# The second feed-forward product as two 64-row halves, between five groups of scores

## The chip, the cores and the metric

One core of a Trainium2 chip runs the whole kernel. The metric is the device time of one execution in microseconds (us), as the median of several runs; lower is better.

## The reference, cut to what matters

The input x is 16 batches of 512 rows of 256 numbers. Each row is normalised (xn). One branch is an attention layer with 16 heads whose scores are a position table, two per-row terms and a small content product; it is followed by a layer norm, a feed-forward network and a second layer norm. The other branch is a gated network whose inputs and weights are rounded to a 4-bit grid. The output is x plus the product of the two branches.

```python
attn = softmax(where(causal, table + qm + km + MIX * qc @ kc.T / sqrt(8), -1e9))
h    = _ln(xn + (attn @ v) @ out_w + out_b, ln1_g, ln1_b)
ffn  = gelu(h @ ffn_w1 + ffn_b1) @ ffn_w2 + ffn_b2     # 256 -> 1024 -> 256
s    = _ln(h + ffn, ln2_g, ln2_b)
g    = silu(fp4_linear(silu(fp4_linear(xn, w_gate)) * fp4_linear(xn, w_up), w_down))
out  = x + s * g
```

The change concerns `gelu(...) @ ffn_w2 + ffn_b2`: a product over 1024 contraction rows.

## The kernel before, in words

After a preamble the work is a loop over 64 steps: 16 batches `b` times four groups `g` of four heads. Line numbers are those of the profile; nearly every instruction carries L72, the line of the helper that records it, so groups are told apart by the names of their tiles.

**What a step does.** Step (b, g) multiplies the weights of the previous step's heads with v (`context`, tile `cp`, L502), then computes, in five bursts, the scores that become the weights of its own four heads (`weights`, tiles `ws`, L466) and the scores whose row maxima the following step needs (`maxima`, tiles `ms`, L427). After the bursts come the gate and up products of one tile of 128 rows of the gated branch (`hidden`, tiles `gp`, `up`, `gu`, L655), the turning of the maxima (`subtracted`, tile `mp`, L442) and the down product of the tile before (`gate`, tile `dp`, L693).

**The batch before rides along.** In steps g = 0 and 1 the previous batch's attention output is projected (`output`, L530). In g = 1 and 2 the first feed-forward product of one half of its rows (two tiles of 128) follows the down product: `expand` (L592) writes eight tiles `act` of 128 hidden units. In g = 2 and 3 `contract` (L603) multiplies them with `w2`: for each of two row tiles, eight products over 128 contraction rows each, all into one PSUM bank `f2` that `biased` (L285) has filled with the bias by a product of ones. `added` (L522) then adds the bank to h on the vector engine and takes the row statistics; `finish` (L621) normalises and writes the output.

**The two sorts of scores.** A score product contracts 36 or 38 rows, so two heads sit in the tensor engine at once, one in rows 0 to 63 and one in rows 64 to 127 (`scores`, L413), each into its own bank. All other products named here use all 128 rows.

**PSUM.** Of the eight banks two belong to a pool `ps_s` with one buffer (the pair `ws`, and later `gu`), one to `cp`, and five to a pool that everything else takes from, in program order and oldest release first. A bank comes free when its reader has run: the vector engine for `ms` (a masked maximum, tile `junk`), `f2` and `up`; the scalar engine for the transposed tiles `xqtp`, `hqtp`, `htp`, which it copies out, and for `gp`, `f1` and `dp`.

**The order.** The order on the tensor, vector and scalar engines is the program's, held by dependencies; only DMA issues and GpSimd are ordered by the scheduler. The program's order within a step is written out in `PLAN` (L711), one string for each g. `W` is a burst of `ws` scores with its exponential on the scalar engine (and a multiplication by the table on GpSimd); `V` is the same with its own two banks of the common pool, one for each head; `M` issues a burst of `ms` scores; `!` puts the maxima of all open `M` and all postponed additions on the vector engine; `f` is two of the sixteen 128-row products of `contract`; `x`, `y` and `h` are transposes of the gated branch's input, its hidden tile (in two parts) and h. The two strings that matter:

```python
"WVM!ffWMM!ffxWM!ffWM!ffyyh", "WMV!ffWMM!ffxWM!fffWM!yfy"   # g = 2 and g = 3
```

Of the kernel before, what the change touches and what calls it, by code (L numbers as in the profile page):

```python
# [17 lines left out]
ALU = mybir.AluOpType  # L18
# [4 lines left out]
B, S, D = 16, 512, 256  # L23
H, M, W, R = 16, 16, 8, 8
# [4 lines left out]
P = 128  # L29
# [21 lines left out]
def tile_block(ctx: ExitStack, tc: tile.TileContext, a: dict, pos: bass.AP, win: bass.AP, out: bass.AP):  # L51
# [22 lines left out]
    pe, dve, act = InOrder(nc.tensor, True), InOrder(nc.vector, False), InOrder(nc.scalar, False)  # L74
# [31 lines left out]
    def statistics(mv, src):  # L106

        st = sb.tile([P, nc.vector.BN_STATS_DIM], F32, name="st", tag="st", bufs=2)
        dve.bn_stats(st, src)
        dve.bn_aggr(mv, st)  # L110

    def inverse_deviation(rs, var):
        nc.gpsimd.tensor_scalar(rs, var, LN_EPS, None, ALU.add)
        nc.gpsimd.tensor_tensor(rs, rs, mhalf[:, : rs.shape[1]], ALU.pow)
# [30 lines left out]
    def layernorm(src, mean, rs, gain, bias):  # L145

        dve.scalar_tensor_tensor(src, src, mean, gain, ALU.subtract, ALU.mult)
        dve.scalar_tensor_tensor(src, src, rs, bias, ALU.mult, ALU.add)
# [29 lines left out]
    NF = D_FF // P  # L178
    w1 = keep.tile([P, NC, D_FF], F32, name="w1", tag="w1")
    w2 = keep.tile([P, NF, D], F32, name="w2", tag="w2")  # L180
    fb1 = keep.tile([P, NF], F32, name="fb1", tag="fb1")

    sums = keep.tile([P, P], F32R, name="sums", tag="sums")
    rows = keep.tile([P, 2, D], F32R, name="rows", tag="rows")
# [61 lines left out]
    def bank(name):  # L246
        return ps.tile([P, 512], F32, name=name, tag="mm")

    mm = pe.matmul

    def turn(dst, src, one=ident):
        pe.transpose(dst, src, one)
# [20 lines left out]
    later = []  # L273

    def caught_up():
        while later:
            later.pop(0)()
# [4 lines left out]
        ((0, 0, 0),), ((1, 0, 0),), ((0, 1, 0), (0, 3, 384)), ((1, 1, 0), (1, 3, 384)), ((0, 2, 0), (1, 2, 256))  # L282
    )

    def biased(acc, i, tiles=2):  # L285

        mm(
            acc[:, : tiles * D].rearrange("p (t d) -> p t d", t=tiles), sums,
            rows[:, i, :].unsqueeze(1).to_broadcast([P, tiles, D]),
            start=True, stop=False, skip_group_check=True,  # L290
        )

    def rows_of(tiles, t):

        return tiles[t // 2][:, t % 2, :]
# [226 lines left out]
    def added(h, tiles, acc, mv):  # L522

        half, at = tiles[0] // 2, tiles[0] % 2
        flat = h[half][:, at : at + len(tiles), :].rearrange("p t d -> p (t d)")
        dve.tensor_tensor(flat, acc[:, : len(tiles) * D], flat, ALU.add)
        for t in tiles:
            statistics(mv[:, t, :], rows_of(h, t))

    def output(b, h, cts, half, mv):  # L530

        cTs, ops = {}, []

        def normal(t):
            tp = bank(f"ctp_{b}_{t}").rearrange("p (h s) -> p h s", s=SLOT)
            for g in range(H // 4):
                turn(tp[:, 4 * g : 4 * g + 4, :].rearrange("p h s -> p (h s)"), cts[g][:, t * P : (t + 1) * P])
            rinv = sb.tile([P, H], F32, name=f"rinv_{b}_{t}", tag="rinv", bufs=2)
            dve.reciprocal(rinv, tp[:, :, HD])
            cx = sb.tile([P, H, HD], F32, name=f"cx_{b}_{t}", tag="cx", bufs=3)  # L540
            dve.tensor_tensor(cx, tp[:, :, 0:HD], rinv.unsqueeze(2).to_broadcast([P, H, HD]), ALU.mult)
            return cx.rearrange("p h d -> p (h d)")

        def turned(t, cx):
            t2 = bank(f"ct2_{b}_{t}")
            for c in range(NC):
                turn(t2[:, c * P : (c + 1) * P], cx[:, c * P : (c + 1) * P])
            cTs[t] = sb.tile([P, D], F32, name=f"cT_{b}_{t}", tag="cx", bufs=3)
            act.copy(cTs[t], t2[:, :D])

        def product(t):
            acc = bank(f"op_{b}_{t}")
            op = acc[:, :D]
            biased(acc, 0, 1)
            cT = cTs[t]
            for c in range(NC):
                mm(op, cT[:, c * P : (c + 1) * P], wo[:, c, :], start=False, stop=(c == NC - 1), skip_group_check=True)
            later.append(lambda: added(h, (t,), acc, mv))

        first, second = 2 * half, 2 * half + 1  # L560
        cx = normal(first)
        yield 0.43
        cx2 = normal(second)
        yield 0.43
        turned(first, cx)
        yield 0.21
        turned(second, cx2)
        yield 0.21
        product(first)
        yield 0.96  # L570
        product(second)
        yield 0.96
# [10 lines left out]
    def turned_h(b, h, half):  # L583
        hT = sb.tile([P, NC, 2 * P], F32, name=f"hT_{b}_{half}", tag="hT")
        tp = bank(f"htp_{b}_{half}")
        for c in range(NC):
            for t in range(2):
                turn(tp[:, (2 * c + t) * P : (2 * c + t + 1) * P], rows_of(h, 2 * half + t)[:, c * P : (c + 1) * P])
        act.copy(hT.rearrange("p c t -> p (c t)"), tp)
        return hT  # L590

    def expand(b, half, hT):  # L592

        acts = []
        for f in range(NF):
            fp = bank(f"f1_{b}_{half}_{f}")
            for c in range(NC):
                mm(fp[:, : 2 * P], w1[:, c, f * P : (f + 1) * P], hT[:, c, :], start=(c == 0), stop=(c == NC - 1))
            acts.append(sb.tile([P, 2 * P], F32, name=f"act_{b}_{half}_{f}", tag="act", bufs=NF + 2))
            act.activation(acts[f], fp[:, : 2 * P], AF.Gelu, bias=fb1[:, f : f + 1])  # L600
        return acts

    def contract(b, h, half, acts, mv, together=2):  # L603

        for first in range(2 * half, 2 * half + 2, together):
            tiles = tuple(range(first, first + together))
            acc = bank(f"f2_{b}_{first}")
            biased(acc, 1, together)
            for i, t in enumerate(tiles):
                at = (t % 2) * P  # L610
                for f in range(NF):
                    mm(
                        acc[:, i * D : (i + 1) * D], acts[f][:, at : at + P], w2[:, f, :],
                        start=False, stop=(f == NF - 1), skip_group_check=True,
                    )
                    if t == tiles[-1] and f == NF - 1:
                        later.append(lambda tiles=tiles, acc=acc: added(h, tiles, acc, mv))
                    if f % 2:
                        yield 0.88

    def finish(b, h, half, mv, gated):  # L621

# [85 lines left out]
        ("r|px|rpp|p|yyr", "pp"),  # L708
        ("p|x||yytt|tt", ""),
    )  # L710
    PLAN = ("WMc!llWM!xWM!ccllyWMlyW!M!l", "WMll!kWM!lWM!xllyhWMccy!WM!l", "WVM!ffWMM!ffxWM!ffWM!ffyyh", "WMV!ffWMM!ffxWM!fffWM!yfy")  # L711

    def keeping(b, g):
        kept(b, g)
# [129 lines left out]
    for c in range(3):  # L844
        at = slice(32 * c, 32 * c + H)
# [148 lines left out]
    for k in range(H // 2 + 2):  # L994
# [20 lines left out]
        if k > 1:  # L1015
            i = k - 2
            row = 2 * M * (i % 4)
            for e in range(2):
                mm(
                    cp[row : row + 2 * M, :], amp[:, 2 * i + e, :], sines[i][:, e, :],  # L1020
                    start=(e == 0), stop=(e == 1), skip_group_check=True,
# [82 lines left out]
    waiting, hq, cts, turned_hs, acts, coming, mv = None, None, [], {}, {}, None, None  # L1104
# [7 lines left out]
    for s in range(STEPS):  # L1112
        b, g = divmod(s, H // 4)
        old, has_old = b - 1, b > 0
# [9 lines left out]
        if has_old:  # L1124
            if g % 2 == 0:
                mv = sb.tile([P, NT, 2], F32, name=f"mv{1 + g // 2}_{old}", tag=f"mv{1 + g // 2}")
# [8 lines left out]
            }  # L1135
            plan = PLAN[g].split("|")
        else:
# [10 lines left out]
        for letter in "".join(part if set(part) & set("WV") else "WM" + "!" * ("!" not in part) + part for part in plan):  # L1148
            if letter in "WV":
                k = next(weighed)  # L1150
# [70 lines left out]
    old = B - 1  # L1221
    h, gated = xns[old], gates[old]
    x_last = load_x(old)
    context(*waiting)
    kept(*waiting[:2])
    mv = sb.tile([P, NT, 2], F32, name="mv1_last", tag="mv1")
    hand = [output(old, h, cts, half, mv) for half in range(2)] + [turned_hidden(*before, hq)]
    for i in (0, 0, 1, 1, 0, 0, 1, 1, 0, 2, 0, 2):
        next(hand[i])
# [11 lines left out]
    mv = sb.tile([P, NT, 2], F32, name="mv2_last", tag="mv2")  # L1241
    for half in range(2):
        acts[half] = expand(old, half, hT)
        if half == 0:
            hT = turned_h(old, h, 1)
        for i, _ in enumerate(contract(old, h, half, acts[half], mv, 1)):
            if i % 4 < 3:
                continue
            caught_up()
            t = 2 * half + i // 4  # L1250
            rs = sb.tile([P, 2], F32, name=f"rs_last_{t}", tag="rs2")
            inverse_deviation(rs[:, :1], mv[:, t : t + 1, 1])
            layernorm(rows_of(h, t), mv[:, t, 0:1], rs[:, :1], g2, b2)
            gt = gated[:, t, :]
            dve.tensor_tensor(gt, gt, rows_of(h, t), ALU.mult)
            dve.tensor_tensor(gt, gt, x_last[:, t, :], ALU.add)
            nc.sync.dma_start(out=out[old, t * P : (t + 1) * P, :], in_=gt)
# [43 lines left out]
```

## Time and profile before

| | |
|---|---|
| Median of 3 runs | 1875.72 us (1874.68 to 1876.05) |
| Profiled execution: span from the first to the last instruction | 1872.6 us |
| Between span and median | 3.1 us |
| PE (tensor engine) busy | 1774.8 us, 95% |
| DVE (vector engine) busy | 1423.1 us, 76% |
| POOL (GpSimd) busy | 1310.3 us, 70% |
| ACT (scalar engine) busy | 1069.1 us, 57% |
| Mean granted clock of the tensor engine | 0.973 |

The profiled execution is known by its span alone; the 3.1 us are what lies around it if it ran as the median did. A single-precision product is two MATMUL passes in the trace, so 16 products show as x32; the scores' type needs one pass. A pass's listed duration is from its issue to the modelled end of its last result, longer than the step from one pass to the next, so the pace of a stage is read from the starts. PEld are the loads of the stationary operand.

The loop is very regular. The steps g = 2 and g = 3 with a previous batch occur 15 times each, the first from 286.5 us, and one of each, at 712.52 and at 741.70 us, is shown below.

### The profile page before, as it was taken

What the parts mean: (1) busy time and instruction counts of PE and PEld (TensorE: products, weight loads), DVE (VectorE), ACT (ScalarE), POOL (GpSimd) and SP (SyncE); (2) the same over time, 40 slices, a digit from 0 to 9 for tenths busy, and PEclk for the clock granted to TensorE, in tenths of its full rate; (3) what the DMA queues carried; (4) which work ended last, traced back from release to release, by engine and by line L of the source; (5) the groups of instructions that cost most, each with busy time, mean ns of one, the idle gap of its engine ahead of it and who ended that gap; (6) DMA issues with size and microseconds to landing.
All of it is one profiled execution on the core that took longest, in us unless ns stands there. A gap on an engine that the chain in (4) does not pass through costs nothing.

```text
span 1872.6 us, 31762 instructions
## 1 busy us (share of the span) xinstructions
PE 1774.8 (95%) x10411; PEld 1240.5 (66%) x10411; DVE 1423.1 (76%) x3887; ACT 1069.1 (57%) x1853; POOL 1310.3 (70%) x1128
## 2 busy tenths in 40 slices
PE   5679799999999999999999999999999999999998
PEld 2235467676776767676776767677676767677676
DVE  5878587787878777787878777787878778787754
ACT  5654455655665555556565565556555565565553
POOL 5467477767776776777676776777677776777671
PEclk8869799999999999999999999999999999999999
DMA  6344242432323242422334242332333242232200
GB/s 203 95 148 134 81 129 68 138 87 88 109 89 120 68 126 80 137 84 76 112 95 127 60 135 81 117 101 76 112 94 109 73 138 86 77 108 79 72 21 12
DMA packets 127114, 184.68 MB, mean 99 GB/s; under 512 B 15315, under 2 KB 57749, under 8 KB 126949
## 3 DMA queue, kind: packets, MB, share of 16 engines
q1 hardware_dynamic: 122496, 181.25, 32.2%
q8 instruction: 83, 1.36, 0.3%
q10 hardware_dynamic: 4004, 0.98, 0.3%
q14 instruction: 83, 0.67, 0.1%
q0 software_dynamic: 448, 0.42, 0.1%
HBM read 136.45 MB, written 45.09 MB: 97 GB/s over the span
## 4 chain that ended last, share of the span: by engine, by line
PE 81%; DVE 8%; POOL 1%; issue 1%; ACT 1%; DMA 0%; DVEq 0%; POOLq 0%; ACTq 0%
PE f L72 25%; PE dp L72 8%; PE gu L72 8%; PE cp L72 7%; PE ws L72 5%; DVE junk L72 4%; PE op L72 4%; PE gp L72 4%; PE up L72 4%; PE ms L72 4%; PE vp L72 3%; PE hqtp L72 2%; DVE cx L72 1%; PE qk_wk L72 1%; PE qk_wq L72 1%
## 5 line engine op out<-in xcount | busy, mean ns | idle before, releaser
L500 POOL TENSOR_TENSOR pr<-pr,table 128x1024 f32<-128x1024 f32 (+2 forms) x448 | 768.0, 1748 | 75.2 <-ACT pr L72 73.0
L72 DVE CUSTOM_DVE_ANT_0 junk<-ms,mask 128x512 bf16<-128x512 f32 (+3 forms) x1024 | 501.9, 490 | 231.9 <-PE ms L72 155.0
L72 ACT ACTIVATE pr<-ws 128x1024 f32<-128x1024 f32 (+1 forms) x350 | 327.0, 955 | 134.4 <-PE ws L72 129.1
L72 ACT ACT_TABLE_LOAD x168 | 215.5, 1283 | 64.3 <-PE gp L72 48.8
L72 PE MATMUL f<-w,act 128*128 128x256 f32 x1024 | 249.0, 387 | 0.0
L72 PE MATMUL f<-hT,w 128*128 128x256 f32 x1024 | 226.3, 380 | 0.0
L72 PEld LDWEIGHTS f<-hT,w 128*128 128x128 f32 x1024 | 194.8, 190 | 26.3 <-ACT hT L72 0.2
L72 PEld LDWEIGHTS f<-w,act 128*128 128x128 f32 x1024 | 187.0, 190 | 31.3
L232 POOL TENSOR_TENSOR wide<-wide,scale 128x704 f32<-128x704 f32 (+1 forms) x71 | 96.6, 1361 | 136.5 <-DVE wide L72 132.9
L72 PE MATMUL ws<-qT,kT 38*128 38x512 f32 (+3 forms) x1024 | 157.5, 371 | 21.4 <-ACT pr L72 16.5
L72 PE MATMUL dp<-wdT,hqT 128*128 128x256 f32 x768 | 176.2, 379 | 0.0
L72 PEld LDWEIGHTS dp<-wdT,hqT 128*128 128x128 f32 x768 | 146.1, 190 | 31.1 <-issue 6.7
L72 ACT ACTIVATE act<-f,fb 128x256 f32<-128x256 f32 x256 | 118.2, 474 | 75.3 <-PE f L72 72.5
L72 PE MATMUL ms<-kT,qT 36*128 36x512 f32 (+3 forms) x1024 | 145.1, 330 | 9.5 <-DMA kT<-k_d 6.3
L72 PE MATMUL cp<-pr,va 128*17 128x512 f32 (+3 forms) x2048 | 151.5, 434 | 0.0
L72 PEld LDWEIGHTS ws<-qT,kT 38*128 38x128 f32 x1024 | 81.6, 188 | 90.8 <-issue 51.7
L72 PEld LDWEIGHTS cp<-pr,va 128*17 128x17 f32 x2048 | 54.3, 97 | 99.4 <-issue 79.5
L223 POOL TENSOR_SCALAR scale<-amax 128x32 f32<-128x32 f32 (+1 forms) x104 | 37.0, 356 | 116.6 <-DVE amax L72 113.5
L72 DVE TENSOR_TENSOR wide<-wide,m 128x704 f32<-128x704 f32 (+2 forms) x126 | 112.4, 892 | 4.1
L222 POOL TENSOR_TENSOR wide<-wide,inv 128x704 f32<-128x704 f32 (+1 forms) x71 | 99.1, 1396 | 21.5 <-DVE inv L72 21.1
L72 PEld LDWEIGHTS ms<-kT,qT 36*128 36x128 f32 x1024 | 96.2, 189 | 18.4 <-issue 12.8
L72 DVE TENSOR_SCALAR m<-m 128x512 f32<-128x512 f32 (+1 forms) x104 | 102.6, 986 | 3.4
(217 smaller groups left out, 3009.5 us busy)
## 6 DMA issues: line engine op xcount, KB each, us to landing
table<-rv SPq DMA_DIRECT2D x64, 1024.0 KB
kT<-k_d SPq DMA_DIRECT2D x256, 76.0 KB
qT<-q_d SPq DMA_DIRECT2D x256, 72.0 KB
x<-in_L_attn_x_dram SPq DMA_DIRECT2D x21, 512.0 KB
q_d<-q_hi SPq DMA_DIRECT2D x32, 256.0 KB
q_d<-q_lo SPq DMA_DIRECT2D x32, 256.0 KB
k_d<-k_hi SPq DMA_DIRECT2D x32, 256.0 KB
k_d<-k_lo SPq DMA_DIRECT2D x32, 256.0 KB
```

Of the source, the lines that this page charges most:

```text
L72: return lambda *args, **kw: self.follow(op(*args, **kw))
L222: nc.gpsimd.tensor_tensor(blocks(dst), blocks(src), per_block(inv), ALU.mult)
L223: nc.gpsimd.tensor_scalar(scale, amax, 1.0 / 6.0, 1e-12, ALU.mult, ALU.max)
L232: nc.gpsimd.tensor_tensor(blocks(dst), blocks(dst), per_block(scale), ALU.mult)
L500: nc.gpsimd.tensor_tensor(part, part, table[:, mine, j * P :], ALU.mult)
```

## The change

`contract` splits each of its products in two along the contraction: rows 0 to 63 into one bank, rows 64 to 127 into a second, in turn. The bias product contracts 64 rows (the rows that hold the bias are among them) and goes into the first bank; the first upper product starts the second. So a step has 32 products of 64 rows in two banks in place of 16 of 128 in one. `added_halves` adds both banks to h, one vector instruction for each, and then takes the statistics as before. The plans of g = 2 and 3 lose `V`, and have four groups `ff` of eight half products between five groups `WM!`; all transposes stand at the end. The last batch's tail keeps whole products, in a function of its own.

```diff
-    def biased(acc, i, tiles=2):
+    def biased(acc, i, tiles=2, n=P):
         mm(
-            acc[:, : tiles * D].rearrange("p (t d) -> p t d", t=tiles), sums,
-            rows[:, i, :].unsqueeze(1).to_broadcast([P, tiles, D]),
+            acc[:, : tiles * D].rearrange("p (t d) -> p t d", t=tiles), sums[:n],
+            rows[:n, i, :].unsqueeze(1).to_broadcast([n, tiles, D]),
             start=True, stop=False, skip_group_check=True,
         )
...
+    def added_halves(h, half, acc, mv):
+        flat = h[half].rearrange("p t d -> p (t d)")
+        for part in acc:
+            dve.tensor_tensor(flat, part, flat, ALU.add)
+        for t in (2 * half, 2 * half + 1):
+            statistics(mv[:, t, :], rows_of(h, t))
...
-    def contract(b, h, half, acts, mv, together=2):
-        for first in range(2 * half, 2 * half + 2, together):
-            tiles = tuple(range(first, first + together))
-            acc = bank(f"f2_{b}_{first}")
-            biased(acc, 1, together)
-            for i, t in enumerate(tiles):
-                at = (t % 2) * P
-                for f in range(NF):
+    def contract(b, h, half, acts, mv):
+        tiles = (2 * half, 2 * half + 1)
+        acc = [bank(f"f2_{b}_{half}_{upper}") for upper in range(2)]
+        biased(acc[0], 1, 2, 64)
+        for i, t in enumerate(tiles):
+            for f in range(NF):
+                for upper in range(2):
+                    k = slice(64 * upper, 64 * upper + 64)
                     mm(
-                        acc[:, i * D : (i + 1) * D], acts[f][:, at : at + P], w2[:, f, :],
-                        start=False, stop=(f == NF - 1), skip_group_check=True,
+                        acc[upper][:, i * D : (i + 1) * D], acts[f][k, i * P : (i + 1) * P], w2[k, f, :],
+                        start=(upper == 1 and i == 0 and f == 0), stop=(f == NF - 1), skip_group_check=True,
                     )
-                    if t == tiles[-1] and f == NF - 1:
-                        later.append(lambda tiles=tiles, acc=acc: added(h, tiles, acc, mv))
-                    if f % 2:
-                        yield 0.88
+                if t == tiles[-1] and f == NF - 1:
+                    later.append(lambda: added_halves(h, half, acc, mv))
+                if f % 2:
+                    yield 0.88
...
-    PLAN = (..., "WVM!ffWMM!ffxWM!ffWM!ffyyh", "WMV!ffWMM!ffxWM!fffWM!yfy")
+    PLAN = (..., "WM!ffWM!ffWM!ffWM!ffWM!xyyh", "WM!ffWM!ffWM!ffWM!ffWM!xyy")
```

In the built program the changed step has this order on the tensor engine: cp; then ws, ms, bias and eight half products; three times ws, ms and eight half products; ws, ms; then xqtp, hqtp (four transposes and two), in g = 2 htp, and gp. The waits that the build attaches to the transposes behind the last burst are: the first of hqtp for the scalar engine (its bank is the one that xqtp leaves), the fifth of hqtp and the first of htp for the vector engine (the two banks of the last `ms`); gp waits in g = 2 for the scalar engine (the bank of the first hqtp) and in g = 3 for the vector engine (the second bank of the last `ms`). The order of the other engines is the same but for the added addition, the one exponential that replaces the two of `V`, the place of the copy of xqtp, which now follows the last exponential, and, in the DMA queue of SP, one load of `kT` for each batch (the last of the group g = 1), which moves from behind the first output store of step g = 3 to ahead of the four small writes of the maxima (L454).

More of the change, by code (lines that the diff above doesn't have):

```diff
@@ L601, in expand, with contract_tile @@
         return acts
-    def contract(b, h, half, acts, mv, together=2):
-        for first in range(2 * half, 2 * half + 2, together):
-            tiles = tuple(range(first, first + together))
-            acc = bank(f"f2_{b}_{first}")
-            biased(acc, 1, together)
-            for i, t in enumerate(tiles):
-                at = (t % 2) * P
-                for f in range(NF):
-                    mm(
-                        acc[:, i * D : (i + 1) * D], acts[f][:, at : at + P], w2[:, f, :],
-                        start=False, stop=(f == NF - 1), skip_group_check=True,
-                    )
-                    if t == tiles[-1] and f == NF - 1:
-                        later.append(lambda tiles=tiles, acc=acc: added(h, tiles, acc, mv))
-                    if f % 2:
-                        yield 0.88
+    def contract(b, h, half, acts, mv):
[6 more added lines that the diff above has]
+                    k = slice(64 * upper, 64 * upper + 64)
+                    mm(
+                        acc[upper][:, i * D : (i + 1) * D], acts[f][k, i * P : (i + 1) * P], w2[k, f, :],
+                        start=(upper == 1 and i == 0 and f == 0), stop=(f == NF - 1), skip_group_check=True,
+                    )
+                if t == tiles[-1] and f == NF - 1:
+                    later.append(lambda: added_halves(h, half, acc, mv))
+                if f % 2:
+                    yield 0.88
+    def contract_tile(b, h, t, acts, mv):
+        acc = bank(f"f2_{b}_{t}")
+        biased(acc, 1, 1)
+        at = (t % 2) * P
+        for f in range(NF):
+            mm(acc[:, :D], acts[f][:, at : at + P], w2[:, f, :], start=False, stop=(f == NF - 1), skip_group_check=True)
+        added(h, (t,), acc, mv)
     def finish(b, h, half, mv, gated):
@@ L710, in tile_block @@
     )
-    PLAN = ("WMc!llWM!xWM!ccllyWMlyW!M!l", "WMll!kWM!lWM!xllyhWMccy!WM!l", "WVM!ffWMM!ffxWM!ffWM!ffyyh", "WMV!ffWMM!ffxWM!fffWM!yfy")
+    PLAN = ("WMc!llWM!xWM!ccllyWMlyW!M!l", "WMll!kWM!lWM!xllyhWMccy!WM!l", "WM!ffWM!ffWM!ffWM!ffWM!xyyh", "WM!ffWM!ffWM!ffWM!ffWM!xyy")
     def keeping(b, g):
@@ L1245, in tile_block @@
             hT = turned_h(old, h, 1)
[L1246 to L1250, printed above, removed]
+        for t in (2 * half, 2 * half + 1):
+            contract_tile(old, h, t, acts[half], mv)
             rs = sb.tile([P, 2], F32, name=f"rs_last_{t}", tag="rs2")
```

## The prediction

> **What bounds the kernel now.** I read the page's busy shares and chain first, then the stretches of two whole steps, then the order of time inside one of them.
>
> ```profile
> PE 1774.8 (95%) x10411; PEld 1240.5 (66%) x10411; DVE 1423.1 (76%) x3887; ACT 1069.1 (57%) x1853; POOL 1310.3 (70%) x1128
> ...
> PE 81%; DVE 8%; POOL 1%; issue 1%; ACT 1%; DMA 0%; DVEq 0%; POOLq 0%; ACTq 0%
> ```
> ```profile
> 712.52:741.70 29.18, 29.18 (x174) 22.00 (x170) 23.07 (x58) 16.61 (x27) 22.48 (x20) 1.00 0.26 77
> 741.70:766.09 24.39, 24.39 (x150) 17.71 (x146) 16.94 (x50) 13.25 (x22) 18.64 (x17) 1.00 0.27 77
> ```
>
> In the steps that change (the first stretch is g = 2, the second g = 3; columns: length, then busy time of PE, PEld, DVE, ACT, POOL, granted clock) the tensor engine is busy for the whole length. They occur 15 times each, so 15 x (29.18 + 24.39) = 804 us are at stake. Busy is not the same as streaming, which the order of time shows:
>
> ```profile
> 703.25 7.07 PE L72 MATMUL f<-hT,w 128*128 128x256 f32 x32
> 710.25 2.35 PE L72 MATMUL cp<-pr,va 128*17 128x512 f32 x32
> 712.52 0.73 PE L72 MATMUL ws<-qT,kT 38*128 38x512 f32 x4
> 713.09 0.39 PE L72 MATMUL ms<-kT,qT 36*128 36x512 f32 x2
> 713.41 0.51 PE L72 MATMUL f<-rows,sums 128*128 128x512 f32 x1
> 713.75 1.89 PE L72 MATMUL f<-w,act 128*128 128x256 f32 x8
> 715.57 0.50 PE L72 MATMUL ws<-qT,kT 38*128 38x384 f32 x4
> ...
> 721.39 0.50 PE L72 MATMUL ws<-qT,kT 38*128 38x256 f32 x4
> 721.74 0.40 PE L72 MATMUL ms<-kT,qT 36*128 36x256 f32 x4
> 722.06 2.00 PE L72 MATMUL f<-w,act 128*128 128x256 f32 x8
> 723.89 0.82 PE L72 MATMUL hqtp<-ident,wide 128*128 128x128 f32 x6
> 724.55 0.60 PE L72 MATMUL htp<-ident,xn 128*128 128x128 f32 x4
> 724.99 1.35 PE L72 MATMUL gp<-wgT,xqT 128*128 128x352 f32 x4
> ...
> 753.69 1.35 PE L72 MATMUL gp<-wgT,xqT 128*128 128x352 f32 x4
> ```
>
> Starts give the pace. 32 passes go from 703.25 to 710.25, the last 0.10 of it idle, so a pass of 256 columns takes 6.90 / 32 = 0.216 us and a group of eight 1.73. The group at 713.75 is followed by scores (64-row tiles) at 715.57, 1.82 later: 0.09 to 0.10 in which the array empties. The group at 722.06 is followed by transposes (128 rows) at 723.89, 1.83 later: 0.10 at its head, where its first weight load had nothing to hide behind. Each crossing between 64-row scores and 128-row work so costs 0.10 + 0.10 = 0.20 us. A pair of score passes of 512 columns takes 0.235: two pairs go from 712.52 to 713.09, less one exposed load.
>
> Step g = 2 reaches gp 12.47 us after its start (724.99 - 712.52), g = 3 after 11.99 (753.69 - 741.70). What follows gp (16.7 and 12.4 us of products without a gap) does not change. So the forecast is two times of gp.
>
> **What the change does to the tensor engine.** Seven crossings ahead of gp in g = 2 become one: all products from the first `ws` to the last `ms` now have 64-row tiles. The 32 half products are 64 passes instead of 32, and cost nothing only if a lower and an upper pass run side by side. No row shows that for single precision in row tiles. The nearest: the scores do it in row tiles with the other type, and cp does it in single precision with four column tiles: its 32 passes hold 40 x 256 columns, 8.6 us at 0.216 one after the other, and take 2.3. I take full overlap; the other end, none, costs 32 x 0.216 = 6.9 us a step.
>
> [...]
>
> Counting from the first `ws` load: load 0.10, ws 0.235, ms 0.235, bias 0.235 (713.41 to 713.75 less a load), hence 0.81; each of four groups of eight half products 1.73; each later ws and ms together 0.47. Burst k = 1 to 4 starts at 2.54, 4.74, 6.94, 9.13; the last `ms` ends at 9.60. If nothing else were late, 0.10 of emptying, 0.10 of load and 12 transposes of 0.109 (hqtp's six go from 723.89 to 724.55) would put gp at 11.1 in g = 2, and eight at 10.7 in g = 3: 1.35 and 1.3 us earlier than now.
>
> **What is late next.** Before, four products stood between the last `ms` and the transposes and hid two waits. Now there is nothing between them, and with `f2` in two of five banks the transposes must take the banks of the last burst.
>
> ```profile
> 712.66 0.59 ACT L72 COPY ct<-cp 128x512 f32<-128x512 f32 x1 [0.32 <-PE cp L72]
> 718.78 0.37 ACT L72 COPY xqT<-xqtp 128x256 f32<-128x256 f32 x1 [1.55 <-PE xqtp L72]
> 722.00 1.02 ACT L72 ACTIVATE pr<-ws 128x1024 f32<-128x1024 f32 x1 [1.76 <-PE ws L72]
> ```
> ```profile
> 713.52 0.69 DVE L72 CUSTOM_DVE_ANT_0 junk<-ms,mask 128x512 bf16<-128x512 f32 x1 [1.53 <-PE ms L72]
> 722.26 0.42 DVE L72 CUSTOM_DVE_ANT_0 junk<-ms,mask 128x256 bf16<-128x256 f32 x1
> 724.12 0.69 DVE L72 TENSOR_TENSOR xn<-f,xn 128x512 f32<-128x512 f32 x1
> ```
>
> Scalar engine, g = 2: the last exponential starts 0.50 after its scores (now 722.00 - 721.39, less the load of 0.10): 9.63. The copy of xqtp is queued behind it, starts at 10.55 (neighbours overlap by 0.1) and ends at 10.92. Only then has hqtp a bank: load and four transposes to the start of their copy take 0.74 (723.89 to 724.53 and 0.10), so 0.05 + 0.74 puts the copy at 11.71; a copy of that shape takes 0.59 (the ct row): 12.30. That frees gp's bank; with 0.05 for the semaphore and 0.10 for the load gp streams at 12.45. Before: 12.47. Gain 0.02.
>
> Vector engine, g = 3: its maxima now wait for each burst. The third burst's are readable at 4.74 + 2 x 0.235 + 0.17 = 5.4; a burst takes the vector engine 2.09, less than the 2.20 between bursts, so the last one begins at 5.4 + 2 x 2.20 = 9.8 and, like the one from 722.26 to 724.2, lasts 1.94: 11.75. Its second bank is gp's: with 0.15 gp streams at 11.90, before 11.99. Gain 0.09. In g = 2 the same event releases htp at 11.8, in time.
>
> So of 1.3 us that the tensor engine saves in a step nearly all becomes this wait.
>
> **The other edits.** The second addition is 0.69 and its gap, 0.72 a step, 21.6 us of vector time in all. It comes behind the last maximum, which ends at 11.75 where it ended at 11.6 (12.4 in g = 3). Cover: the vector engine ends a step 1.5 us and more before its first `ms` is ready (the [1.53] above), and nothing on PE before the next step's second burst waits for what is late. Cost nothing; uncovered it would be 0.72 x 30 = 22 us. One exponential of 1024 columns replaces two of 512 (2 x 0.6 by its tile's list), on an engine with room: nothing. The table products on GpSimd run back to back for 12 us from the first exponential; with bursts 2.2 apart and 2.4 us of work in each it stays fed, and cp needs the last one ten microseconds later: nothing. The moved `kT` load is one issue of 0.3 us on SP ahead of writes that the next step needs ten microseconds later: nothing. The tail of the last batch is as before.
>
> [...]
>
> **Sum.** 15 x (0.02 + 0.09) = 1.7 us. Span 1872.6 - 1.7 = 1870.9, with the 3.1 us around it 1874.0. That is within 0.2% of the median, 3.75 us, about the smallest change a measurement of this kernel tells from none.
>
> **Rivals.** (a) The waits behind the last burst do not bind: the full 1.35 + 1.3 us per batch come through, 40 us, 1836. For: the tensor engine carries 81% of the chain. Against: the build's waits and the two sums above. 6%. (b) Slower, by the bank chain: since gp now follows the last burst by a fixed 3.3 us, whatever stretches a group of half products moves gp one for one. With 0.10 at each of the eight changes between scores and half products (half a crossing; the type changes there, though the tile does not) it is 0.8 x 30 = 24 us, 1898. From 0.13 us a step on it decides. Against: bias to products changes type now and shows no more than its load. 22%. (c) Slower, without overlap: 6.9 x 30 = 207, 2080. 8%. My case: 64%.
>
> **Range and chances.** In my case each time of gp may be wrong by 0.2, 6 us in all: 1868 to 1880. To leave out no more than 2 in 10 the range takes most of (b): 1868 to 1897. Within 0.2%, 0.50 (most of my case, a little of b). Faster by more, 0.13: (a) and half of what my case leaves. Slower by more, 0.37: (c), most of (b), the other half of it and some more, as unlisted waits cost time only.
>
> **What would show it.** Right: half products with starts 0.216 apart in pairs, no idle array between bursts, gp near 12.4 and 11.9, idle of hqtp and gp put down to ACT (xqT, hqT) and DVE (mx), steps of 29.1 and 24.3 us, f<-w,act near 1984 passes. Wrong: half products 0.43 apart for a pair (c), gaps at the changes of type (b), gp near 11.1 (a), or PE waiting within the bursts for `ms` banks.

## The result and the profile after

The changed kernel takes 1885.36 us (median of 4 runs, 1884.69 to 1887.24) where the kernel before takes 1875.2: ratio on record 1.0059, 95% interval 1.0045 to 1.0073. It is 10 us slower; 1874.0 was predicted. The profiled execution has a span of 1883.3 us, 10.7 more than before.

The page first, busy shares and chain:

```profile
PE 1756.6 (93%) x11371; PEld 1254.7 (67%) x11371; DVE 1447.5 (77%) x3917; ACT 1068.0 (57%) x1823; POOL 1316.8 (70%) x1128
...
PE 78%; DVE 8%; ACT 4%; issue 1%; POOL 1%; DVEq 0%; POOLq 0%; ACTq 0%
```

The tensor engine is busy 18 us less and the span is longer; the scalar engine's share of the chain rises from 1% to 4%. Next whole steps, columns as in the prediction (length; busy time of PE, PEld, DVE, ACT, POOL; granted clock): a g = 1, the g = 2 and the g = 3 behind it, and another g = 1.

```profile
686.18:714.70 28.52, 27.98 (x183) 20.37 (x179) 24.28 (x65) 17.96 (x31) 19.68 (x16) 1.00 0.43 130
714.70:744.10 29.40, 28.47 (x207) 22.35 (x204) 24.00 (x59) 16.55 (x26) 22.50 (x20) 1.00 0.25 76
744.10:768.60 24.50, 23.57 (x182) 18.14 (x179) 17.53 (x51) 13.19 (x21) 19.35 (x17) 1.00 0.26 73
1007.13:1037.19 30.06, 29.50 (x183) 21.50 (x179) 24.28 (x65) 18.16 (x31) 19.35 (x16) 0.94 0.38 119
```

Two things have grown. Steps g = 2 and 3 went from 29.18 and 24.39 to 29.39 and 24.51 (means over the batches): 15 x (0.21 + 0.12) = 4.9 us. And some steps g = 1, which the change does not touch, last 30.06 in place of 28.52, at a mean granted clock of 0.94. In the clock record of the trace these are windows of 3.41 us at half clock, each worth 1.55 us. The kernel before has three of them in the loop (from 261.6, 688.2 and 1432.3 us), the changed one six (262.0, 477.0, 797.9, 1012.9, 1333.8, 1654.6): 3 x 1.55 = 4.6 us. Together 9.5 of the 10.7. The rest is 0.4 ahead of the second batch, 0.4 in one step g = 0 (24.39 in place of 24.03) and 0.3 in the last step g = 1; why is open.

Inside the g = 2 step from 714.70 (start, then busy time and group), tensor engine and then scalar engine:

```profile
715.28 0.39 PE L72 MATMUL f<-rows,sums 64*128 64x512 f32 x1
715.28 1.90 PE L72 MATMUL f<-w,act 64*128 64x256 f32 x15
...
717.02 0.38 PE L72 MATMUL f<-w,act 64*128 64x256 f32 x1
...
719.22 0.38 PE L72 MATMUL f<-w,act 64*128 64x256 f32 x1
...
719.62 0.22 PE L72 MATMUL ws<-qT,kT 38*128 38x128 f32 x1
...
719.74 0.43 PE L72 MATMUL f<-w,act 64*128 64x256 f32 x1
...
721.53 0.38 PE L72 MATMUL f<-w,act 64*128 64x256 f32 x1
...
722.04 0.43 PE L72 MATMUL f<-w,act 64*128 64x256 f32 x1
...
723.83 0.38 PE L72 MATMUL f<-w,act 64*128 64x256 f32 x1
...
724.61 0.44 PE L72 MATMUL xqtp<-ident,xq 128*128 128x128 f32 x2
725.98 0.85 PE L72 MATMUL hqtp<-ident,wide 128*128 128x128 f32 x6 [0.93 <-ACT xqT L72]
726.72 0.66 PE L72 MATMUL htp<-ident,xn 128*128 128x128 f32 x4
727.28 1.45 PE L72 MATMUL gp<-wgT,xqT 128*128 128x352 f32 x4
```
```profile
724.55 1.02 ACT L72 ACTIVATE pr<-ws 128x1024 f32<-128x1024 f32 x1 [1.34 <-PE ms L72]
725.47 0.37 ACT L72 COPY xqT<-xqtp 128x256 f32<-128x256 f32 x1
726.64 0.86 ACT L72 COPY hqT<-hqtp 128x512 f32<-128x512 f32 x2 [0.81 <-PE hqtp L72]
```

The halves overlap: the bias product and the first pass of a half product start together (715.28), and from there pairs of passes start up to 17 ns apart every 0.2155 us. (The first pair behind a pass of 128 columns is 40 to 49 ns apart, and in one step of the last batch pairs are 33 to 35 apart.) The rows do not say which half a pass belongs to; the bias product sits in the lower rows, and I take the pass that starts with it for an upper one, so that the upper half stays one pass ahead. By this reading one lower pass is left alone at the end of each group, and its times (717.02, 719.22, 721.53, 723.83) are the clock of the step: 2.20, then 2.31 and 2.30 apart. A burst has both halves when that pass has run, 0.2155 later: 2.54, 4.74, 7.05 and 9.35 us behind the step's start. Behind the last burst the array waits 0.93 us for the copy of xqT, as it was predicted in kind.

### The profile page after: what moved, and what is told of

Its sections match the earlier page's. It is cut to its first block, busy times and chain, and to the rows that moved or that the text cites. A ratio compares the mean times of both kernels' runs of the same rounds, so it can differ in the third digit from the quotient of the medians.

```text
span 1883.3 us, 33721 instructions
## 1 busy us (share of the span) xinstructions
PE 1756.6 (93%) x11371; PEld 1254.7 (67%) x11371; DVE 1447.5 (77%) x3917; ACT 1068.0 (57%) x1823; POOL 1316.8 (70%) x1128
## 3 DMA queue, kind: packets, MB, share of 16 engines
q8 instruction: 90, 1.47, 0.3%
## 4 chain that ended last, share of the span: by engine, by line
PE 78%; DVE 8%; ACT 4%; issue 1%; POOL 1%; DVEq 0%; POOLq 0%; ACTq 0%
PE f L72 23%; PE dp L72 8%; PE gu L72 8%; PE cp L72 7%; PE ws L72 4%; PE op L72 4%; PE gp L72 4%; PE up L72 4%; DVE junk L72 3%; PE ms L72 3%; PE vp L72 3%; PE hqtp L72 3%; ACT pr L72 2%; PE qk_wk L72 1%; PE qk_wq L72 1%
## 5 line engine op out<-in xcount | busy, mean ns | idle before, releaser
L72 ACT ACTIVATE pr<-ws 128x1024 f32<-128x1024 f32 x320 | 328.2, 1026 | 187.4 <-PE ms L72 110.1
L72 PE MATMUL f<-w,act 64*128 64x256 f32 (+1 forms) x1984 | 270.6, 379 | 0.0
L72 PEld LDWEIGHTS f<-w,act 64*128 64x128 f32 (+1 forms) x1984 | 215.0, 186 | 20.2
L72 PE MATMUL ws<-qT,kT 38*128 38x512 f32 (+3 forms) x1024 | 200.2, 397 | 20.3 <-ACT pr L72 15.4
L72 PE MATMUL ms<-kT,qT 36*128 36x128 f32 (+3 forms) x1024 | 172.8, 329 | 10.2 <-DMA kT<-k_d 7.0
L72 PEld LDWEIGHTS ws<-qT,kT 38*128 38x128 f32 x1024 | 113.1, 190 | 68.5 <-ACT pr L72 32.4
L72 PEld LDWEIGHTS ms<-kT,qT 36*128 36x128 f32 x1024 | 118.4, 189 | 18.2 <-issue 14.4
```

The lines of the kernel that those rows point to most:

```text
L72: return lambda *args, **kw: self.follow(op(*args, **kw))
```

## The experiments

The theory: half of the loss is gp, held by the fixed chain of banks and copies behind a last burst that comes 0.2 us late; the other half is the clock, by more half-clock windows in untouched steps. Rivals: the second addition's time on the vector engine; a cost inside the half products; windows that come by chance. In the table, the period is that of a batch without half-clock loss, and the windows are those in the steps g = 1 of batches 1 to 14, both from the profiled run. The ratios are those on record, each against runs of the kernel before in the same series (medians 1874.6 to 1875.4), and not quotients of the medians shown.

| Kernel | Median, us | Ratio to before (95%) | Period, us | Windows |
|---|---|---|---|---|
| before | 1874.6 (25 runs) | | 106.11 | 3 |
| changed | 1885.4 | 1.0059 (1.0045 to 1.0073) | 106.44 | 6 |
| before_pad034 | 1881.1 | 1.0041 (1.0029 to 1.0054) | 106.47 | 4 |
| after_pad277 | 1918.9 | 1.0233 (1.0219 to 1.0246) | 109.27 | 1 |
| after_one_add | 1868.5 | 0.9962 (0.9950 to 0.9974) | 105.02 | 7 |
| after_whole | 1910.9 | 1.0185 (1.0172 to 1.0198) | 107.93 | 9 |
| after_small_add | 1884.3 | 1.0046 (1.0033 to 1.0058) | 106.44 | 6 |
| before_fill | 1878.6 | 1.0020 (1.0011 to 1.0029) | 106.53 | 0 |
| after_fill | 1882.2 | 1.0039 (1.0026 to 1.0051) | 106.90 | 0 |
| after_x_first_fill | 1876.4 | 1.0008 (0.9999 to 1.0017) | 106.27 | 0 |
| after_x_first | 1870.9 | 0.9975 (0.9965 to 0.9985) | 105.84 | 1 |
| before_c | 1872.4 | 0.9985 (0.9977 to 0.9994) | 106.21 | 0 |
| after_x_first_c | 1872.5 | 0.9989 (0.9980 to 0.9998) | 105.95 | 0 |
| after_x_first_f_c | 1883.1 | 1.0042 (1.0029 to 1.0055) | 106.84 | 0 |

### Does the batch period set the number of half-clock windows?

**before_pad034**, in `gate` of the kernel before:

```diff
         dp = bank(f"dp_{b}_{t}")
+        if b and t == 2:
+            for n in [200]:
+                mm(dp[:, :n], hqT[:, 0, :], wdT[:, 0, :n], start=True, stop=True, skip_group_check=True)
```

> The kernel before, with one product over 200 columns done twice in the down product of every step g = 3 (15 times): 0.337 us of tensor time a batch at the pace of 0.431 for 256 columns, which brings the batch period (106.11 us) to that of the changed kernel (106.44). Theory: the half-clock windows of 3.41 us come at fixed multiples of that length, fall into the thin part of a step g = 1 by the phase against the batch, and their number follows the batch period. Going through the 15 batches with a period of 106.44 and an end of the preceding window between 5.0 and 5.8 us behind the start of a step g = 1 as the condition gives about 5 or 6 such windows in place of 3, 1.5 us each: 5.1 + 3 to 5 = 8 to 10 us, 1883 to 1885, with half-clock records near those of the changed kernel (262, 477, 798, 1013, 1334, 1655). Rival (the windows of the changed kernel come from its changed steps, or by chance): 5.1 us, 1880, with 3 windows at other times.

1881.05: 6.3 above the 1874.8 that the kernel before took beside it, between the two expectations. The six runs are far apart, four at 1880.0 to 1881.4 (mean granted clock 0.973 to 0.974) and two at 1886.5 and 1887.1 (0.968), so the half-clock time differs from run to run. The period was as meant (106.47), but the profiled run has four windows, at 582.1, 903.0, 1118.0 and 1438.9, not at the times of the changed kernel: the grid on which the windows lie met the loop at another place (these four lie 0.3 us ahead of a whole multiple of 3.4133 from the 261.57 of the kernel before). It tells little by itself.

**after_pad277**: the same lines in the changed kernel with `[256] * 6 + [110]`.

> The changed kernel, with 2.77 us of repeated products in the down product of every step g = 3 (six products of 256 columns at 0.431 and one of 110 at 0.185), so that the batch period becomes 109.21 us, 32 windows of 3.413. Theory of the phase: one half-clock window in a step g = 1 at the start of the loop and one at its end, none between, in place of six and one: 15 x 2.77 = 41.5, less 5 x 1.55 = 7.7: 33.8 us above the changed kernel, 1919. Rival (number of windows independent of the period): 1927, with six.

1918.86, as the theory said and 8 us below the rival. With a period of 32 windows (109.27 against 32 x 3.4133 = 109.23) the grid stays put: one window at the start of the loop and none after it.

Taken over 98 steps g = 1 of the first seven kernels of the table, in which this step is the same: a half-clock window follows when an edge of the 3.413 us grid lies 4.62 to 5.81 us behind the step's start (36 steps), and does not at 4.07 to 4.67 or 5.81 to 7.34 (62 steps). The grid is read from the clock records: in the traces of the kernel before and of the changed one every half-clock record starts a whole multiple of 3.4133 us from the others of its trace, to within 0.01, and the shortest last 3.412 to 3.413. So in this step the place of the edge tells whether a window follows. The 3.41 us ahead of such an edge hold a thin stretch of scores and transposes with small gaps: ahead of the window at 1012.91 of the changed kernel these are 0.20 and 0.30 us in front of `ct` and 0.05 in front of ws, 0.55 together, all that the step has. None is over 0.30, and a half-clock window still follows. Which of these sets it off, no run tells.

**before_fill** and **after_fill** put full work into that stretch, in both kernels:

```diff
         tp = bank(f"xqtp_{b}_{t}")
+        if b and t == 1:
+            mm(tp[:, :D], ident, w1[:, 0, :D], start=True, stop=True, skip_group_check=True)
```

> The kernel before, with one idle product (128 rows, 256 columns, overwritten by the transposes that follow) ahead of xqtp in each of the 15 steps g = 1, in front of a wait of 0.30 us. It streams for 0.43, so the step should become 0.13 longer. Theory: the half-clock windows come where a window of 3.41 us lies over the thin part of this step, so with 0.43 us more of full work in it none is set off there any more: 15 x 0.13 = 2 less 3 x 1.5 = 4.5, 1872, and no half-clock record between 265 and 1740. Rival (the windows have nothing to do with how thin this stretch is): 1877 with two to four of them.

> The same idle product in the changed kernel. Theory: no half-clock window from 265 to 1740, 15 x 0.13 = 2 less 6 x 1.55 = 9.3: 1878. Against the filled kernel before, 5 to 6 us are left, which is what the steps g = 2 and 3 became longer by (15 x (0.21 + 0.12) = 4.9). Rival: 1887, and 10 us of distance to the filled kernel before.

The windows are gone from both loops, and not because the grid moved out of the way: eight of the 28 steps g = 1 still have an edge of the grid 4.6 to 5.8 us behind their start, and no window follows. The step g = 1 of the filled changed kernel (columns as above):

```profile
1005.65:1034.61 28.96, 28.30 (x187) 20.67 (x183) 24.27 (x65) 17.98 (x31) 19.34 (x16) 1.00 0.42 124
```

28.96 is 0.44 more than 28.52: the idle product costs its whole length, and not 0.13 as I expected, since the wait behind it moved along instead of shrinking (the tensor engine idles 28.96 - 28.30 = 0.66 us in the step, and 0.54 without the product). So the kernel before lost 15 x 0.44 = 6.6 against three windows and got slower (1878.6, above both expectations), and the changed one, with six to avoid, got faster. The distance between the two shrinks from 10.2 to 3.7 us; their steps g = 2 and 3 still differ by 0.22 and 0.13 (29.39 and 24.51 against 29.17 and 24.38), 15 x 0.35 = 5.2, and the filled kernel before has more half-clock time in its last batch (13.6 us of records against 3.4).

**before_c** reaches the same without added work: the v product comes earlier in g = 1.

```diff
-    PLAN = (..., "WMll!kWM!lWM!xllyhWMccy!WM!l", ...)
+    PLAN = (..., "WMll!kWM!lcWM!xllyhWMcy!WM!l", ...)
...
+            if t == (1 if b > 1 else 0):
+                per_row()        # the products of m, from ahead of the loop over t
+                yield 0.43
             vp = bank(f"vp_{b}_{t}")
```

> The kernel before, with one v product (vp, 0.86 us of full 128-row work that the step holds anyway) moved inside g = 1 from behind the fourth burst to ahead of the third, for batches from the second on; the small products of m follow where it stood. No work is added. Theory: full work in the thin stretch means no half-clock window from 265 to 1740, and xqtp and the second ct no longer wait 0.30 us: 1875.3 - 3 x 1.5 - (0 to 15 x 0.3) = 1866 to 1871. Rival (the bank that vp takes and the later third burst hold up the vector engine, which is nearly full there): up to 0.86 a step, 1884.

No window in the loop; the step is 28.63, 0.11 longer than 28.52 rather than 0.3 shorter, so that 1.6 of the 4.6 us go again. It is faster than the kernel before by 0.15%.

### The second addition, or the second bank?

**after_one_add**: `for part in acc[:1]` in `added_halves`.

> The changed kernel without the addition of the second bank: the upper halves of the products are computed but left out of the output. Theory: the second addition has cover on the vector engine and costs nothing: 1885, within 3 us, steps g = 2 and 3 of the same length. Rival: it is what holds the transposes' or gp's banks, 0.72 x 30 = 21.6 us back, 1864; or a part of it.

1868.47: 17 us less than the changed kernel. That looked like the rival, until the order of time showed where it came from:

```profile
932.54 0.44 PE L72 MATMUL xqtp<-ident,xq 128*128 128x128 f32 x2
932.81 0.60 PE L72 MATMUL hqtp<-ident,wide 128*128 128x128 f32 x4
933.82 0.44 PE L72 MATMUL hqtp<-ident,wide 128*128 128x128 f32 x2 [0.40 <-ACT xqT L72]
934.09 0.60 PE L72 MATMUL htp<-ident,xn 128*128 128x128 f32 x4
934.53 1.05 PE L72 MATMUL gp<-wgT,xqT 128*128 128x352 f32 x3
```

hqtp starts 0.27 behind xqtp, where it starts 1.37 behind in the changed kernel (724.61 to 725.98): here the bank that nobody reads was free at once. The two steps are 28.61 and 23.85, 15 x (0.78 + 0.66) = 21.6 us less.

**after_small_add** keeps the bank's reader and takes its time away:

```diff
-        for part in acc:
-            dve.tensor_tensor(flat, part, flat, ALU.add)
+        dve.tensor_tensor(flat, acc[0], flat, ALU.add)
+        dve.tensor_tensor(flat[:, :8], acc[1][:, :8], flat[:, :8], ALU.add)
```

> The changed kernel with its second addition cut to 8 of 512 columns, so that the second bank still has a reader at the same place but the vector engine's time for it is nearly gone; the rest of the upper halves is left out of the output. The kernel without any second addition came out 17 us faster, with hqtp streaming right behind xqtp instead of waiting 0.9 us. Theory: that was the bank, which without a reader was free for hqtp, and not the addition's time: here 1885, within 2 us, the wait of 0.93 in steps g = 2 and 3 is back. Rival (the 0.69 of vector time is on the path): 1864 to 1870.

1884.32, steps of 29.39 and 24.50, the 0.93 us of waiting back. The addition is free; the bank is worth 21.6 us.

### What do the halves save, under the same order?

**after_whole**: `contract` of the kernel before in the changed one, new plan kept.

> The changed kernel's order of bursts and groups, but with the whole products over 128 rows in one bank as before (one bias product of 512 columns, one addition). Eight crossings between 64-row and 128-row work in a step in place of one, each put at 0.20 us: the last burst starts 1.4 us later than in the changed kernel, and as all behind it (exponential, xqT, hqtp, hqT, gp) is a fixed chain, gp follows one for one: 15 x 2.8 = 42 us, less some 6 us of half-clock windows that a batch period of 109.24 (32 windows) avoids: 1921. Rival (the crossings' cost is hidden behind the wait at the end, or is not removed by the halves): 1885 to 1895.

1910.91, 25.5 above the changed kernel and 10 below what I expected. Its last burst and what follows, in a step that began at 942.76:

```profile
953.47 0.50 PE L72 MATMUL ws<-qT,kT 38*128 38x256 f32 x4
953.81 0.40 PE L72 MATMUL ms<-kT,qT 36*128 36x256 f32 x4
954.14 0.44 PE L72 MATMUL xqtp<-ident,xq 128*128 128x128 f32 x2
954.41 0.60 PE L72 MATMUL hqtp<-ident,wide 128*128 128x128 f32 x4
955.41 0.44 PE L72 MATMUL hqtp<-ident,wide 128*128 128x128 f32 x2 [0.40 <-ACT xqT L72]
```

The burst starts at 953.47 - 942.76 = 10.71 by its record, and its first load of 0.10 is exposed: 10.81 in place of 9.35. The transposes behind it say the same, 954.14 - 942.76 = 11.38 in place of 724.61 - 714.70 = 9.91. That is 1.47 us for seven crossings, 0.21 each, about as priced. But with one bank held and not two, hqtp does not wait for xqT, and the steps of 30.08 and 25.33 are only 0.69 and 0.82 longer than the changed kernel's. So of the 1.47 us that the halves save ahead of the transposes, about 0.78 and 0.65 are lost again behind them, which I had left out. It is what the kernel without the second addition gained (0.78 and 0.66): the price of the second bank, found twice. The windows did not become fewer either: the period came out at 107.93 and not 109.24, with nine of them. Steps and windows make 15 x 1.51 + 3 x 1.55 = 27, where 25.5 were measured.

### Out of the chain

**after_x_first_fill** and **after_x_first** (the second without the idle product):

```diff
-    PLAN = (..., "WM!ffWM!ffWM!ffWM!ffWM!xyyh", "WM!ffWM!ffWM!ffWM!ffWM!xyy")
+    PLAN = (..., "xWM!ffWM!ffWM!ffWM!ffWM!yy", "xWM!ffWM!ffWM!ffWM!ffWM!yy")
...
         next(halves)
+        if has_old and g == 2:
+            turned_hs[1] = turned_h(old, xns[old], 1)
```

> The filled changed kernel, with xqtp moved from behind the last burst to ahead of the first in steps g = 2 and 3, and htp of g = 2 moved behind the first gate and up products. Theory (gp waits for banks and the chain exponential, xqT copy, hqtp, hqT copy): hqtp gets the third free bank at once, some 10.1 us into the step, its copy follows the last exponential and ends near 11.5, gp streams at 11.6 in place of 12.68 (g = 2) and 12.11 (g = 3): 15 x (1.0 + 0.5) = 22 us less than the filled changed kernel, 1856. Rival (gp is held by the last maxima on the vector engine at about 12.0 in both): 15 x (0.7 + 0.1) = 12 us less, 1866; or the scalar engine's first exponential, now behind the copy of xqT, holds up the second burst: no gain.

> xqtp ahead of the first burst and htp behind up as in the kernel of that kind with the idle product, without the idle product. Its batch period of 106.27 us becomes 105.84, and 31 windows of 3.413 are 105.81. Theory: the phase of the windows then hardly moves from batch to batch, so after one or two half-clock windows at the start it stays where none is set off: 1876.4 - 15 x 0.43 + 0 to 3 = 1870 to 1873. Rival (without the idle product the thin stretch of g = 1 sets off six of them, as in the changed kernel): 1879.

With xqtp ahead of the first burst hqtp has its bank at once. The steps are 29.02 and 24.27, so 15 x (0.37 + 0.24) = 9 us less in the loop, 5.8 by the median; 22 or 12 were expected. (The profiled run has 17.1 us of half-clock records in its last batch, the filled changed kernel 3.4.) I had read the gain from the time of gp alone, and xqtp (0.37) and htp (0.44) were only moved, so the tensor engine still has to do them; the wait fell from 0.93 to 0.41. Without the idle product the batch is 105.84 us, 31 windows to within 0.03, and the grid stands still as foretold: one window at 263.0 and then none until the last batch. 1870.85 is 0.25% faster than the kernel before (0.15 to 0.35%) and the fastest of those that compute the whole output.

**after_x_first_c** adds the earlier v product; **after_x_first_f_c** also moves the last `f` behind the last burst (`"xWM!ffWM!ffWM!ffWM!fWM!fyy"` in both steps).

> The changed kernel with xqtp ahead of the first burst, htp behind up, and vp moved as above. Theory: no half-clock windows, no idle product: 1876.4 - 6.5 - (0 to 4.5) = 1865 to 1870, faster than the kernel before by 0.3 to 0.5%. Rival (as for vp in the kernel before): 1883.

> As the one above, with the last four products (eight half products, 0.86 us) moved behind the last burst. In the kernel with xqtp first hqtp's second part still waits 0.41 us in each step for a bank of the last maxima; the vector engine idles 0.31 just ahead of them. Theory (gp follows the last burst by a fixed chain, here the maxima's): the last maxima can come 0.3 earlier and no more, the wait shrinks to 0.1: 15 x 2 x 0.3 = 9 us less than the one above, 1857 to 1861. Rival (the hqT copy behind the last exponential is what gp waits for, and both move by 0.86): 15 x 2 x 0.4 = 12, and all of the wait gone; or no gain at all, if the vector engine has no room.

The first, 1872.49 where 1865 to 1870 was expected, gains nothing on 1870.85: there were no windows left to avoid, and the moved product costs its 0.11 a batch. The second loses 10.6: the steps are 29.47 and 24.71. Counted from the last cp pass, the maxima of the last burst end at 12.35 where they ended at 12.52: the vector engine is busy with those of the burst before until 10.27 and starts the next 0.14 later, as between all its pairs, so 0.17 is all the room it had. And gp, which in the other kernel got a bank that the scalar engine frees and started at 11.97, now has a bank of these maxima and starts at 12.41. Neither the theory nor its rival saw that the assignment of banks turns with the order.

## Why the prediction was wrong

- **Crossings, 0.20 each.** Right: 1.47 us for seven, 0.21 each.
- **Full overlap of the halves.** Right: pairs of passes start every 0.2155, and the first two bursts behind the bias start at 2.54 and 4.74, as in the sum. One half does trail by a pass, but by the bias product, whose 0.235 the sum held. Rival (c) is out.
- **The count from burst to burst, "each later ws and ms together 0.47".** This term failed. With 1.73 for a group the bursts should be 2.20 apart; they are 2.20, 2.31 and 2.30. Those with passes of 384 and 128 columns take 0.58. By columns they are as long as one of 512; a pass of 128 lasts 0.06 (719.62 to 719.68), less than the 0.10 of an exposed load, and by my reading leaves a part of the load behind it exposed. The rows agree: the first half product behind such a pass is listed with 0.43 (719.74, 722.04) where the others have 0.38. With whole products the burst is longer by only half as much (0.05), as there the second short pass stands ahead of a crossing, where the load is exposed anyway. That reading fits the size, but no run tested it by itself. The last burst starts at 9.35 and not at 9.13.
- **What is late next.** Right in mechanism and length. From the last burst to gp the sum had 12.45 - 9.13 = 3.32, the trace has 12.68 - 9.35 = 3.33 (gp's record at 12.58 and its exposed load of 0.10). In g = 3 the vector engine's maxima end at 11.95, predicted 11.75, and gp streams at 12.11, predicted 11.90. So the banks do not return at fixed times: they follow the last burst. Each 0.2 of the wrong count came through one for one: 15 x (0.23 + 0.21) = 6.6 us, which turns a gain of 1.7 into a loss of 4.9. This is the leverage that rival (b) named; I put its stretch at the changes of type, where there is none, and priced it at 24 us. The range was widened to 1897 for that price; that 1885 lies in it is luck. Two small terms of the sum had no row beside them. The 0.05 for a semaphore is in both traces (before: from the end of an exponential at 685.71 to the load of the ws that waited for it, 685.76). The 0.17 from a burst's last pass to its maxima is 0.19 before (the last ms pass starts 0.42 ahead of the maximum at 713.52 and takes 0.235).
- **The second addition at nothing.** Right; but the second bank, which the text named and did not price by itself (it is inside the forecast wait), is 21.6 us.
- **The unlisted half.** 4.6 us come from half-clock windows in steps that the change does not touch. The prediction had three of them in its trace and did not ask what they depend on. (Of the 0.027 that the mean clock of 0.973 lacks, most lies before 230 us, in the preamble and the first batch: 82 us of half-clock records there, 10 in the three windows.) The grid shifts against the batch by the period less 31 x 3.413 = 105.81, so by 0.30 us a batch before and by 0.63 after. One passage is 3.41, of which a window with its 1.55 jumps a part. By this estimate one comes in every (3.41 - 1.55) / 0.30 = 6 batches before and in every 3 after; in the traces they lie 4 and 7 batches apart before, 2 or 3 after.

## What to carry to other kernels

When a chain of fixed length hangs behind the last piece of a group, price that piece's start to 0.05 us, each shape by its own rows, because nothing behind it forgives. Count banks as a resource of their own: here splitting a product into two accumulators cost 21.6 us for the second bank, where the addition that came with it cost nothing. And before trusting a difference under 1%, look at the granted clock step by step: untouched steps that differ may be a cost of the loop's period, and not of the work that the change does.

## What the hardware showed that I had not expected

- The half-clock windows lie on a grid of 3.413 us, and in the steps g = 1 they come over a thin stretch with no gap over 0.30 us; with an idle product of 0.43 us in it none came (after_fill 0 in place of 6, before_fill 0 in place of 3). In the changed kernel their number went with the batch period: six at 106.44 us, one at 109.27 (after_pad277); as the spread between runs suggests, it may also go with where the grid meets the loop. In the profiled runs 0.33 us a batch so cost 0.33 + 0.31.
- Batch and grid locked in one kernel. In the one without the second addition a window came in every second batch, 211.6 us apart (474.5, 686.1, 897.8, 1109.4, 1321.0, 1532.6): two batches of 105.02 and one loss of 1.55 make 62 windows. Of its 21.6 us of shorter steps 17 were left.
- In the changed kernel two single-precision passes in different row halves start up to 17 ns apart (a few up to 49) and take the time of one (0.2155 us for a pair of 256 columns). The bias product of one half, in the other type, and a pass of the other half run side by side too (both from 715.28, the next pair from 715.50).
